# Nucleus search on one core: the next search's bracket inside the tie branch, the next logits' maxima after round two, and scaled results of S put into the attention groups

## The chip, the cores and the metric

The kernel runs on one core of one Trainium2 chip. The metric is device time in microseconds (us). An execution with the hardware profiler gives the trace; its own time is given beside its span.

## The reference, cut to what matters

Layer 0 is a graph attention over N = 2708 nodes with D = 512 features and 8 heads. Layer 1, which the change is about, runs two steps of a diffusion with three streams:

```
S = adj + I;  Rf = S / rowsum;  Rb = S / colsum
for s in (0, 1):
    logits = (Xa W1) W2 (Xa W3)^T                    # N x N
    order each row by falling logits; csum = cumulative softmax
    keep the first k_i = #(csum < 0.9) + 1 of the row  # "nucleus"
    A  = softmax of the kept logits, 0 elsewhere
    Xf = Rf Xf;  Xb = Rb Xb;  Xa = A Xa
    Z += Xf U1[s] + Xb U2[s] + Xa U3[s]
out = x + layernorm(X + Z) * gamma + beta
```

The kernel does not sort. For each row it searches for the threshold above which the sum of exp(logit - max) just reaches 0.9 of the total.

## The kernel before, in words

Rows lie in 22 tiles of 128 partitions, and two tiles make a pair, so a step has eleven pairs, 0 to 10. Two pairs make a quad. The two steps are the two passes of one outer loop; "step one" is s = 0, "step two" is s = 1 (`last` in the code).

For each pair the work runs through these stages.

- `Logits.products` (L534, L536): TensorE forms the logits of the pair in chunks, ScalarE copies each chunk from PSUM into the tile p. The pool holds four p tiles, two pairs, so the copies of pair g+2 wait until the search of pair g has finished with its p.
- `Logits.exp`: VectorE takes the rows' maxima (L561, two reductions over 2708 elements). It returns a list of further steps for ScalarE and GpSimd ("fills"): a sum with half the exponent (`root`), the exponential (`full`), three trial thresholds from these sums by GpSimd (`points`, L578-L588), and twelve passes of ScalarE over the rows (L566, "looks") that give the masses above the three thresholds; GpSimd puts them together (`masses`, L591-L593, the tile pts).
- `search`: VectorE forms a bracket around the threshold from the three masses (L637-L666, tiles g0, ends, below), then does rounds of a secant search, each with one pass over each row tile (L642): two in step one, four in step two. After that it picks out the next largest values (L819, L821), forms `keep` (the kept exponentials, L743 or L748-L751), and tests for ties.
- `branch`: the test's result is packed into the integer code_i (L900), loaded into a register of the VectorE queue (L901), and a switch of five arms follows (L903). Arm 0 is empty, arms 1 to 3 mend ties in one or both tiles (L760-L770), arm 4 does more rounds. After the switch stands the reciprocal rden (L920).
- `attended`: TensorE transposes keep in groups of four 128x128 blocks (L1069), ScalarE copies each group out of PSUM (tile at, L1073), TensorE multiplies by va (L1087), which holds Xa. A tile has six groups, a pair twelve. ScalarE scales the result by rden (L1095).
- In step one, `mixed` multiplies the result by U3 and writes it out. In step two GpSimd adds z to it (L1097), which holds what the other streams gave, and `normed` normalizes the rows: statistics by VectorE (L137, L138), two operations by VectorE (L1150, L1151) and a store on GpSimd's queue (L1152).
- `part` gives the products with S as a list of steps ("others"): in step one S by [Xf, Xb] (which start as the same X) and through U1 and U2; in step two S by the streams (L983), through U (L1004), and at the end of each half of a quad four calls of `summed`, one for each tile: ScalarE scales a PSUM bank into xe (L1027, two buffers), GpSimd adds that to z (L1029). The first half of a quad also loads z (SP's queue).

The order on TensorE, ScalarE, VectorE and SP is written out by hand; `paced(steps, n)` does the next n steps of a list. GpSimd's order is the scheduler's. Iteration g of the loop does the products of pair g+2, the attention of pair g on TensorE and ScalarE, the search of pair g+1 on VectorE, the fills of pair g+2 between the attention's groups, and part g+2 of the S products:

```
for g in range(-1, NP):
    others = part(half, g + 2)
    if g + 2 < NP: lg[g + 2].products()
    ...
    if g >= 0: att = attended(pairs[g], *ready, fills, others, ...)
    def early(g=g):                      # called by search after its first round
        if g + 2 < NP: fills.extend(lg[g + 2].exp())
        return lambda: [rest() for rest in norms] + [paced(pending, len(pending))]
    def late(g=g):                       # called by search before its selection
        if g >= 0: out_ = rest_of(att); ...
            while others or fills: paced(others, 2); paced(fills, 1)
    ready = search(lg[g + 1], g >= 0, early, late)
```

So the four results of `summed` are done at the end of an iteration, ahead of the next products.

Of the kernel before, what the change touches and what calls it, by code (L numbers as in the profile page):

```python
# [24 lines left out]
P = 128  # L25
LEAKY_ALPHA = 0.2
LN_EPS = 1e-5
P_NUC = 0.9
# [25 lines left out]
def kernel(  # L54
# [553 lines left out]
                steps.append(masses)  # L608
            return steps

    def search(lg, looked, early, late):
# [6 lines left out]
        tiles = [(i, rows[t]) for i, t in enumerate(grp)]  # L618
        junk = wide.tile([P, -(-N // 4) * 2], F32, name="junk", bufs=1)
        junk_b = junk.bitcast(BF16)[:, :N]  # L620
# [8 lines left out]
        ends = vec("ends", 2, 3)  # L629
        cur = vec("cur", 3)  # L630
        th = vec("th")
        g0 = vec("g0")
        if lg.ragged:
            v.memset(cur, 0.0)

        def aim(dst, th):
            v.scalar_tensor_tensor(dst, th, AIM[s], lg.cap, op0=OP.mult, op1=OP.min)  # L637
            v.scalar_tensor_tensor(dst, tot, 1.0 - P_NUC + CURVE, dst, op0=OP.mult, op1=OP.add)
            v.reciprocal(dst, dst)

        def mass(i, pr, th, dst):
            v.scalar_tensor_tensor(junk_b[:pr], ps_[i][:pr], th, ps_[i][:pr],  # L642
                                   op0=OP.is_ge, op1=OP.mult, accum_out=dst)

        if not looked:
            for j in range(NA):
                for i, pr in tiles:
                    mass(i, pr, lg.th[:pr, j, i:i + 1], lg.pts[:pr, j, 2, i:i + 1])
        aim(g0, lg.th[:, NA // 2])
        v.tensor_scalar(ends[:, 0, 1], tot, CURVE, None, op0=OP.mult)  # L650
        v.tensor_copy(ends[:, 1, 1], lg.top)
        v.reciprocal(ends[:, :, 1], ends[:, :, 1])
        v.tensor_tensor(ends[:, :, 1], ends[:, :, 1], g0.unsqueeze(1).to_broadcast([P, 2, G]), op=OP.subtract)
        v.memset(ends[:, 0, 0], X_LO)
        v.memset(ends[:, 1, 0], X_HI)
        v.tensor_copy(ends[:, 0, 2], tot)
        v.memset(ends[:, 1, 2], 0.0)
        pg = lg.pts[:, :, 1]
        v.tensor_tensor(pg, lg.top.unsqueeze(1).to_broadcast([P, NA, G]), lg.pts[:, :, 2], op=OP.subtract)
        v.reciprocal(pg, pg)  # L660
        v.tensor_tensor(pg, pg, g0.unsqueeze(1).to_broadcast([P, NA, G]), op=OP.subtract)
        below = vec("below", 2, NA, dtype=I32)
        for e, order, op in ((0, range(NA), OP.is_ge), (1, reversed(range(NA)), OP.is_lt)):
            v.tensor_scalar(below[:, e], pg, 0.0, None, op0=op)
            for j in order:
                v.copy_predicated(ends[:, e], below[:, e, j].unsqueeze(1).to_broadcast([P, 3, G]), lg.pts[:, j])  # L666
        side = vec("side", 2, dtype=I32)
        d = vec("d", 2)
        fr = vec("fr")

        def rounds(n, aim_at=None):
            for it in range(n):
                v.tensor_tensor(d, ends[:, 1, 0:2], ends[:, 0, 0:2], op=OP.subtract)
                v.tensor_scalar(d[:, 1], d[:, 1], -1e-12, None, op0=OP.min)
                v.reciprocal(fr, d[:, 1])
                v.tensor_mul(fr, fr, ends[:, 0, 1])
                v.tensor_scalar(fr, fr, -0.95, -0.05, op0=OP.max, op1=OP.min)
                v.tensor_mul(fr, fr, d[:, 0])
                v.tensor_tensor(cur[:, 0], ends[:, 0, 0], fr, op=OP.subtract)
                v.tensor_mul(th, cur[:, 0], cur[:, 0])  # L680
                v.tensor_mul(th, th, th)
# [203 lines left out]
        def branch(go):  # L885
# [8 lines left out]
            for q in range(4):  # L894
# [3 lines left out]
            v.scalar_tensor_tensor(flag_t[0:1, 0:G + 1], flag_t[0:1, 0:G + 1], 1.0, weights[0:1], op0=OP.mult,  # L898
                                   op1=OP.mult, accum_out=code[0:1])
            v.tensor_scalar(code_i[0:1], code[0:1], float(1 << G), None, op0=OP.min)  # L900
            what = nc.values_load(code_i[0:1, 0:1], engines=[DVE], min_val=0, max_val=1 << G,  # L901
                                  skip_runtime_bounds_check_because="at most 1 << G")
            for arm in tc.Switch({DVE: what}, (1 << G) + 1):  # L903
                if 0 < arm < 1 << G:
                    ties([x for x in tiles if arm >> x[0] & 1])
                elif arm == 1 << G and go == 0:
                    rounds(MORE_ROUNDS)
                    choose()
                    finish(1)
                elif arm == 1 << G and go == 1:  # L910
                    v.copy_predicated(th, short, vn[:, :, nx - 1])
                    v.copy_predicated(kept[:, 1], short, den)
                    finish(2)
                elif arm == 1 << G:
                    bisect()

        late()
        finish(0)
        rden = small.tile([P, G], F32, name="rden1")
        v.reciprocal(rden, den)  # L920
        return keep, rden

    big = ctx.enter_context(tc.tile_pool(name="big", bufs=1))
    va = big.tile([P, NT, D], F32, name="va")
# [2 lines left out]
    for s in range(STEPS):  # L927
        last = s == STEPS - 1
        with ExitStack() as st:
# [128 lines left out]
            def attended(grp, keep, rden, fills, others, first=3):  # L1058
# [94 lines left out]

                return rest

            def ranks():
# [5 lines left out]
                junk = wide.tile([P, -(-N // 4) * 2], F32, name="junk", bufs=1).bitcast(BF16)[:, :N]  # L1162
# [42 lines left out]
            pools = (wide, small, ps_t)  # L1205
            NP = len(pairs)
            with tc.manual_schedule(engines={PE, ACT, DVE, SP}):
                counted, spread = ranks() if last else (None, None)
                lg = [Logits(pools, s, grp, keys, rank) for grp in pairs[:1]]
                lg[0].queries()  # L1210
                lg[0].products()
# [9 lines left out]
                    step()  # L1221
                values()
                done = []
                ready = None
                looks = []
                for g in range(-1, NP):

                    fills = []
# [1 line left out]
                    others = part(half, g + 2)  # L1230
                    if g + 2 < NP:
                        lg[g + 2].products()
                    if g + 3 < NP:
                        lg.append(Logits(pools, s, pairs[g + 3], keys, rank))
                        lg[g + 3].queries()
# [17 lines left out]
                    def late(g=g):  # L1253
                        if g >= 0:
# [65 lines left out]
```

## Time and profile before

| | |
|---|---|
| median of 3 runs | 3685.08 us (3682.25 to 3693.7) |
| profiled execution | 3677.84 us, span 3676.0 us |
| busy, share of the span | PE 91%, DVE 72%, ACT 41%, POOL 24% |
| granted TensorE clock, mean | 0.962 |

PE is TensorE's matmul side, DVE VectorE, ACT ScalarE, POOL GpSimd, SP the queue of most loads. Layer 0 takes about the first 1090 us; step one's attention runs from about 1226 to 2300 us and step two's from about 2482 us on. A line such as "DVE nmx L561 <- ACT p L536" says that an instruction of line 561, which writes nmx, came to run when ScalarE's line 536 had written p; "issue" stands for time in which the engine waited for nothing that the profile shows.

### The profile page before, as it was taken

To read this page: it belongs to the slowest core of one execution; us is meant where nothing else is said; L and a number is where in the kernel's file an instruction comes from. 1 tells how busy PE (TensorE), PEld (TensorE's weight loads), DVE (VectorE), ACT (ScalarE), POOL (GpSimd) and SP (SyncE) were. 2 spreads that over 40 slices of the span, in tenths; PEclk is the share of its full clock that TensorE was granted. 3 is DMA by queue.
4 is the path that set the end of the run, shared out by engine and by line. 5 is a ranking of instruction groups with operands and counts; after the bars stand their busy time and mean duration, and the time that the engine had idled before them with its cause. 6 is when DMAs were issued, how large, how long until landed. Compare 5 with 4: busy or idle time off the path is not lost. (4 is left out here: it accounts for less than half of the span.)

```text
span 3676.0 us, 34194 instructions
## 1 busy us (share of the span) xinstructions
PE 3337.2 (91%) x10791; PEld 1723.9 (47%) x10791; DVE 2662.3 (72%) x4832; ACT 1504.8 (41%) x2248; POOL 873.0 (24%) x1072
## 2 busy tenths in 40 slices
PE   7998999998867799999999999879898999999887
PEld 4433333333444454646455553555455555555443
DVE  4587888989965557455464751887888998888884
ACT  2343212011113666565665641337444563545610
POOL 4114241514321012221122221311212222122211
PEclk9999999999979899999999999989999999999988
DMA  4476424233227344536254343874356444564442
GB/s 115 158 245 238 147 74 159 74 110 100 81 81 283 136 151 149 189 103 216 77 182 159 139 159 99 288 250 140 129 192 212 162 161 161 201 221 169 142 156 102
DMA packets 247978, 580.17 MB, mean 158 GB/s; under 512 B 33305, under 2 KB 67049, under 8 KB 243491
## 3 DMA queue, kind: packets, MB, share of 16 engines
q1 hardware_dynamic: 226695, 503.59, 41.0%
q0 software_dynamic: 21040, 73.88, 5.2%
q8 instruction: 86, 1.41, 0.2%
q14 instruction: 157, 1.29, 0.1%
HBM read 471.68 MB, written 105.68 MB: 157 GB/s over the span
## 5 line engine op out<-in xcount | busy, mean ns | idle before, releaser
L1087 PE MATMUL a<-va,at 128*128 128x512 f32 (+2 forms) x1936 | 893.5, 601 | 15.3 <-ACT at L1073 14.9
L442 PE MATMUL po<-e,fw 128*65 128x512 f32 (+4 forms) x2112 | 839.9, 553 | 34.2 <-DVE e L440 23.5
L440 DVE SCALAR_TENSOR_TENSOR e<-r_b,kk,a_c 128x512 f32<-128x512 f32 (+4 forms) x1056 | 751.3, 740 | 70.6 <-PE po L442 19.9
L566 ACT ACTIVATE junk_a<-p,nth 128x2708 uint8<-128x2708 f32 (+1 forms) x240 | 612.7, 2553 | 106.2 <-POOL nth L585 102.0
L983 PE MATMUL q<-hl,s_r 128*128 128x512 f32 x1936 | 524.1, 419 | 59.4 <-DMA s_r<-s_d 59.0
L442 PEld LDWEIGHTS po<-e,fw 128*65 128x65 f32 (+1 forms) x2112 | 285.8, 140 | 548.7 <-issue 270.5
L1087 PEld LDWEIGHTS a<-va,at 128*128 128x128 f32 (+2 forms) x1936 | 339.1, 187 | 390.0 <-issue 340.5
L983 PEld LDWEIGHTS q<-hl,s_r 128*128 128x128 f32 x1936 | 361.6, 191 | 211.9 <-issue 59.9
L642 DVE SCALAR_TENSOR_TENSOR junk<-p,th 128x2708 bf16<-128x2708 f32 (+1 forms) x132 | 409.7, 3103 | 3.8
L1004 PE MATMUL q<-u_k,tt 128*128 128x512 f32 x704 | 319.9, 597 | 9.6 <-DMA u_k<-in_L_gnn_U_dram 9.6
L1073 ACT COPY at<-t 128x512 f32<-128x512 f32 (+3 forms) x308 | 140.5, 477 | 438.9 <-PE t L1069 438.1
L986 PE MATMUL q<-s_r,hl 128*128 128x512 f32 (+1 forms) x1056 | 281.0, 410 | 10.9 <-DMA s_r<-s_d 10.7
L534 PE MATMUL t<-keys,q_t 128*128 128x452 f32 x528 | 166.8, 447 | 110.9 <-ACT p L536 97.4
L986 PEld LDWEIGHTS q<-s_r,hl 128*128 128x128 f32 x1056 | 186.7, 188 | 99.3 <-issue 52.0
L1004 PEld LDWEIGHTS q<-u_k,tt 128*128 128x128 f32 x704 | 134.8, 192 | 160.9 <-issue 156.7
L561 DVE TENSOR_REDUCE nmx<-p 128x1 f32<-128x2708 f32 (+1 forms) x44 | 129.6, 2969 | 99.1 <-ACT p L536 99.1
L821 DVE MAX8 vn<-keep 128x8 f32<-128x2708 f32 (+1 forms) x66 | 196.8, 2981 | 2.3
L536 ACT COPY p<-t 128x452 f32<-128x452 f32 (+2 forms) x264 | 132.7, 537 | 133.7 <-PE t L534 106.7
L534 PEld LDWEIGHTS t<-keys,q_t 128*128 128x128 f32 x528 | 94.9, 215 | 180.2 <-ACT p L536 153.0
L424 ACT ACTIVATE s_c<-a_c 128x512 fp32r<-128x512 f32 (+3 forms) x132 | 76.2, 577 | 244.9 <-DMA a_c<-in_adj_t_dram 118.6
L1127 PE MATMUL a<-u_k,v_t 128*128 128x512 f32 (+1 forms) x352 | 169.5, 618 | 1.9 <-DMA u_k<-in_L_gnn_U_dram 1.8
L1069 PE MATMUL t<-ident,keep 128*128 128x128 f32 (+1 forms) x968 | 147.8, 275 | 23.9 <-DVE keep L770 11.3
(305 smaller groups left out, 3362.3 us busy)
## 6 DMA issues: line engine op xcount, KB each, us to landing
s_r<-s_d SPq DMA_DIRECT2D x330, 256.0 KB
hl<-vhl_d SPq DMA_DIRECT2D x132, 512.0 KB
hl<-fhl_d SPq DMA_DIRECT2D x132, 512.0 KB
hl<-bhl_d SPq DMA_DIRECT2D x132, 512.0 KB
u_k<-in_L_gnn_U_dram SPq DMA_DIRECT2D x184, 256.0 KB
arow<-in_adj_dram SPq DMA_DIRECT2D x21, 1354.0 KB
s_d<-s_c SPq DMA_DIRECT2D x88, 256.0 KB
a_c<-in_adj_t_dram SPq DMA_DIRECT2D x84, 256.0 KB
```

The lines of the kernel that those rows point to most:

```text
L440: nc.vector.scalar_tensor_tensor(e[:pr, :cw], r_b[:pr, i, :cw], kk[:pr, t, hd:hd + 1], a_c[t][:pr, :cw], op0=OP.max, op1=OP.mult)
L442: nc.tensor.matmul(po[i][:, :cw], lhsT=fw[:pr, t, hd, :], rhs=e[:pr, :cw], start=(t == 0), stop=(t == NT - 1))
L534: nc.tensor.matmul(pl[:, :c1 - c0], lhsT=q[:, i], rhs=self.keys[:, c0:c1], start=(i == 0), stop=(i == 1))
L566: nc.scalar.activation(junk[:pr], self.p[i][:pr], func, **kw)
L642: v.scalar_tensor_tensor(junk_b[:pr], ps_[i][:pr], th, ps_[i][:pr], op0=OP.is_ge, op1=OP.mult, accum_out=dst)
L821: v.max(vs, keep[0][:pr])
L983: nc.tensor.matmul(half[j], lhsT=s_r[:, j * P:(j + 1) * P], rhs=hl[:, h], start=(c == 0 and h == 0), stop=(c == NT - 1 and h == 1))
L986: nc.tensor.matmul(half[j][:, :w], lhsT=hl[:, h, j * P:(j + 1) * P], rhs=s_r[:, :w], start=(c == 0 and h == 0), stop=(c == NT - 1 and h == 1))
L1004: nc.tensor.matmul(half[j], lhsT=across_t[-1][:, k, j * P:(j + 1) * P], rhs=u_k, start=(start and k == 0), stop=(start and k == KD - 1))
L1069: nc.tensor.transpose(pt[:rows[c], j, :pr], keep[i][:pr, cols[c]], ident[:pr, :pr])
L1087: nc.tensor.matmul(pa[:pr], lhsT=at[:rows[c], j, :pr], rhs=va[:rows[c], c, :], start=(c == 0), stop=(c == NT - 1))
L1127: nc.tensor.matmul(pz[i][:rows[t]], lhsT=v_t[i][:, k, :rows[t]], rhs=u_k, start=(k == 0), stop=(k == KD - 1))
```

## The change

Three edits, as the description of the change has them.

1. The tiles of the bracket move into a class `Opened`, in two parts: `ready` (the subtraction that needs the masses, and the curve at the middle threshold, g0) and `bracket` (all the rest). For pairs 2 to 10 `ready` of the next pair is issued between code_i and its load, and `bracket` at the end of each of the five arms. For pairs 0 and 1 both stay in front of the search. The small tiles get two buffers, and junk is allocated once a step.
2. `early` is called after round `s` rather than after round 0: in step two the next pair's maxima come after the second round, and with them the rest of `normed` moves ahead of the third round. In step one nothing moves.
3. In step two up to four last steps of `others` (the calls of `summed`) are left over at the end of an iteration, and the next iteration's attention does one of them in each of its groups from the second on.

```diff
+    class Opened:
+        def __init__(self, lg, looked, junk):
...
+            if looked:
+                self.ready()
...
+        def ready(self):
+            v, lg = nc.vector, self.lg
+            if lg.ragged:
+                v.memset(self.cur, 0.0)
+            pg = lg.pts[:, :, 1]
+            v.tensor_tensor(pg, lg.top.unsqueeze(1).to_broadcast([P, NA, G]), lg.pts[:, :, 2], op=OP.subtract)
+            self.aim(self.g0, lg.th[:, NA // 2])
+        def bracket(self):
...
+            for e, order, op in ((0, range(NA), OP.is_ge), (1, reversed(range(NA)), OP.is_lt)):
+                v.tensor_scalar(below[:, e], pg, 0.0, None, op0=op)
+                for j in order:
+                    v.copy_predicated(ends[:, e], below[:, e, j].unsqueeze(1).to_broadcast([P, 3, G]), lg.pts[:, j])
...
-                if it == 1 and begun:
+                if begun:
                     begun.pop()()
...
-                if it == 0 and aim_at is not None:
+                if it == s and aim_at is not None:
                     begun.append(early())
...
             v.tensor_scalar(code_i[0:1], code[0:1], float(1 << G), None, op0=OP.min)
+            opened = None
+            if go == 0 and then:
+                opened = then()
             what = nc.values_load(code_i[0:1, 0:1], engines=[DVE], min_val=0, max_val=1 << G,
...
                 elif arm == 1 << G:
                     bisect()
+                if opened:
+                    opened.bracket()
...
                     nxt = turned(*steps[n + 1]) if n + 1 < len(steps) else None
+                    if n:
+                        paced(left, 1)
                     if n >= first:
...
-                    rk_t = small.tile([NT, P], BF16, name="rk_t", bufs=1)
+                    rk_t = sp.tile([P, 2 * G * P], F32R, name="s_r").bitcast(BF16)[:NT, :P]
...
-                            while others or fills:
-                                paced(others, 2)
+                            keeps = min(len(others), len(quads[g // 2 + 1])) if last and others else 0
+                            while len(others) > keeps or fills:
+                                paced(others, min(2, len(others) - keeps))
                                 paced(fills, 1)
+                            left.extend(others)
+                            others.clear()
                             return
...
-                        ready = search(lg[g + 1], g >= 0, early, late)
+                        if g == 0:
+                            opened = Opened(lg[1], True, junk)
+                            opened.bracket()
+                        then = (lambda g=g: Opened(lg[g + 2], True, junk)) if 0 <= g < NP - 2 else None
+                        ready, opened = search(lg[g + 1], opened, junk, early, late, then)
```

More of the change, by code (lines that the diff above doesn't have):

```diff
@@ L609, in exp, with vec, aim, mass @@
             return steps
-    def search(lg, looked, early, late):
+    class Opened:
+        def __init__(self, lg, looked, junk):
+            _, small, _ = lg.pools
+            self.lg, self.looked = lg, looked
+            self.tiles = [(i, rows[t]) for i, t in enumerate(lg.grp)]
+            self.junk_b = junk.bitcast(BF16)[:, :N]
+            def vec(name, *shape, dtype=F32):
+                return small.tile([P, *shape, G], dtype, name=name, bufs=2)
+            self.ends = vec("ends", 2, 3)
+            self.cur = vec("cur", 3)
+            self.th = vec("th")
+            self.g0 = vec("g0")
+            self.below = vec("below", 2, NA, dtype=I32)
+            self.side = vec("side", 2, dtype=I32)
+            self.d = vec("d", 2)
+            self.fr = vec("fr")
+            if looked:
+                self.ready()
+        def aim(self, dst, th):
+            v, lg = nc.vector, self.lg
+            v.scalar_tensor_tensor(dst, th, AIM[lg.s], lg.cap, op0=OP.mult, op1=OP.min)
+            v.scalar_tensor_tensor(dst, lg.tot, 1.0 - P_NUC + CURVE, dst, op0=OP.mult, op1=OP.add)
+            v.reciprocal(dst, dst)
+        def mass(self, i, pr, th, dst):
+            p = self.lg.p[i][:pr]
+            nc.vector.scalar_tensor_tensor(self.junk_b[:pr], p, th, p, op0=OP.is_ge, op1=OP.mult, accum_out=dst)
+        def ready(self):
+            v, lg = nc.vector, self.lg
+            if lg.ragged:
[4 more added lines that the diff above has]
+        def bracket(self):
+            v, lg = nc.vector, self.lg
+            ends, g0 = self.ends, self.g0
+            v.tensor_scalar(ends[:, 0, 1], lg.tot, CURVE, None, op0=OP.mult)
+            v.tensor_copy(ends[:, 1, 1], lg.top)
+            v.reciprocal(ends[:, :, 1], ends[:, :, 1])
+            v.tensor_tensor(ends[:, :, 1], ends[:, :, 1], g0.unsqueeze(1).to_broadcast([P, 2, G]), op=OP.subtract)
+            v.memset(ends[:, 0, 0], X_LO)
+            v.memset(ends[:, 1, 0], X_HI)
+            v.tensor_copy(ends[:, 0, 2], lg.tot)
+            v.memset(ends[:, 1, 2], 0.0)
+            pg = lg.pts[:, :, 1]
+            v.reciprocal(pg, pg)
+            v.tensor_tensor(pg, pg, g0.unsqueeze(1).to_broadcast([P, NA, G]), op=OP.subtract)
+            below = self.below
+            for e, order, op in ((0, range(NA), OP.is_ge), (1, reversed(range(NA)), OP.is_lt)):
+                v.tensor_scalar(below[:, e], pg, 0.0, None, op0=op)
+                for j in order:
+                    v.copy_predicated(ends[:, e], below[:, e, j].unsqueeze(1).to_broadcast([P, 3, G]), lg.pts[:, j])
@@ L615, in search @@
+    def search(lg, o, junk, early, late, then=None):
         (wide, small, _), grp, ps_, tot, thr, s = lg.pools, lg.grp, lg.p, lg.tot, lg.thr, lg.s
@@ L617, in search @@
         nx = NEXT[s]
-        tiles = [(i, rows[t]) for i, t in enumerate(grp)]
-        junk = wide.tile([P, -(-N // 4) * 2], F32, name="junk", bufs=1)
-        junk_b = junk.bitcast(BF16)[:, :N]
+        begins = o is None
+        if begins:
+            o = Opened(lg, False, junk)
+            for j in range(NA):
+                for x in o.tiles:
+                    o.mass(*x, lg.th[:x[1], j, x[0]:x[0] + 1], lg.pts[:x[1], j, 2, x[0]:x[0] + 1])
+            o.ready()
+            o.bracket()
+        tiles, aim, mass = o.tiles, o.aim, o.mass
+        ends, cur, th, g0, side, d, fr = o.ends, o.cur, o.th, o.g0, o.side, o.d, o.fr
+        junk_b = o.junk_b
         keep = [wide.tile([P, N], F32, name="keep") for _ in tiles]
@@ L624, in vec @@
             return small.tile([P, *shape, G], dtype, name=name, bufs=1)
[L629 to L669, printed above, removed]
         def rounds(n, aim_at=None):
@@ L915, in branch @@
                     bisect()
+                if opened:
+                    opened.bracket()
+            if go == 0:
+                nxt.append(opened)
+        nxt = []
         late()
@@ L920, in search @@
         v.reciprocal(rden, den)
-        return keep, rden
+        return (keep, rden), nxt[0]
     big = ctx.enter_context(tc.tile_pool(name="big", bufs=1))
@@ L1154, in normed, with ranks @@
                 return rest
-            def ranks():
+            def ranks(junk):
                 same = wide.tile([P, N], F32, name="keep")
                 mask = wide.tile([P, N], F32, name="keep").bitcast(BF16)[:, :(NT + 1) * P]
-                junk = wide.tile([P, -(-N // 4) * 2], F32, name="junk", bufs=1).bitcast(BF16)[:, :N]
                 own = small.tile([P, NT], F32, name="own", bufs=1)
@@ L1207 @@
             with tc.manual_schedule(engines={PE, ACT, DVE, SP}):
-                counted, spread = ranks() if last else (None, None)
+                junk = wide.tile([P, -(-N // 4) * 2], F32, name="junk", bufs=1)
+                counted, spread = ranks(junk.bitcast(BF16)[:, :N]) if last else (None, None)
                 lg = [Logits(pools, s, grp, keys, rank) for grp in pairs[:1]]
@@ L1223 @@
                 done = []
-                ready = None
-                looks = []
+                ready = opened = None
+                looks, left = [], []
                 for g in range(-1, NP):
@@ L1232 @@
                         lg[g + 2].products()
+                    if g < 0:
+                        paced(left, len(left))
                     if g + 3 < NP:
```

## The prediction

> **What bounds the kernel now.** I read the stages first, then the waits by stage, then the timeline at the places where one pair of row tiles follows another. A step handles eleven pairs, 0 to 10. The table of stages (us, then busy time of each engine) for step one from its pair 2 on, for the head of step two, and for the rest of step two:
>
> ```profile
> 1330.00:2130.00 800.00, 770.85 (x2513) 419.45 (x2514) 445.71 (x948) 491.94 (x611) 149.49 (x242) 0.98 0.42 145
> 2475.00:2850.00 375.00, 330.61 (x1116) 197.02 (x1114) 313.36 (x588) 198.00 (x223) 72.52 (x76) 0.95 0.48 165
> 2850.00:3420.00 570.00, 532.37 (x1823) 316.99 (x1824) 484.55 (x909) 288.93 (x331) 142.72 (x129) 0.99 0.53 180
> ```
>
> Step one is TensorE's: PE is busy 96%, DVE 56%. In step two PE has 88%, then 93%, and DVE 84% and 85%. There the two hold each other: ScalarE may copy the products of pair g+2 (L536) only when search g has left its branch, since they reuse its p buffers, and search g+1 needs those copies for its maxima (L561). What PE and DVE wait for in step two (us in total, times, longest; from the waits of two windows, 2560 to 3450 and 2475 to 3520):
>
> ```profile
> PE t L534 <- ACT p L536: 48.1, 23, 14.5
> ```
>
> ```profile
> DVE rden L920 <- issue: 50.6, 8, 7.6
> DVE nmx L561 <- ACT p L536: 27.3, 8, 7.0
> DVE pts L659 <- POOL pts L593: 26.4, 1, 26.4
> ```
>
> PE's wait is not the same everywhere. Before attention of pair 1 PE stands 12.95 us, before pair 3 14.5 us: DVE is late (pair 3 has ties). Before pairs 2 and 4 to 8 it stands 2.7 to 5.1 us in all, and DVE had left its branch 2 to 15 us earlier. There ScalarE's four scaled results, which wait for POOL's adds, stand in front of the copies:
>
> ```profile
> 3180.15 1.27 ACT L1027 ACTIVATE xe<-q,cinv 128x512 f32<-128x512 f32 x2 [30.46 <-PE q L983]
> 3182.24 0.69 ACT L1027 ACTIVATE xe<-q,cinv 128x512 f32<-128x512 f32 x1 [0.83 <-POOL z L1029]
> 3183.46 0.69 ACT L1027 ACTIVATE xe<-q,cinv 128x512 f32<-128x512 f32 x1 [0.53 <-POOL z L1029]
> 3184.05 0.97 ACT L536 COPY p<-t 128x452 f32<-128x452 f32 x2
> ```
>
> Last, the branch. From the end of code_i to rden DVE sits idle, here 6.4 us (4.6 to 7.6 over the searches without ties):
>
> ```profile
> 3159.63 0.14 DVE L900 TENSOR_SCALAR code_i<-code 1x1 int32<-1x1 f32 x1
> 3166.16 0.17 DVE L920 RECIPROCAL rden<-den 128x2 f32<-128x2 f32 x1 [6.39 <-issue]
> ```
>
> The sequencer's own records split this: the load and the jump into arm 0 end at 3161.0 with a prefetch hint, 1.2 us after code_i; the exit jump follows at 3161.3, and 4.9 us pass. Where an arm ran ties for 17 us, rden came 0.8 us after it[...]. In step one the exit takes 3.3 us (1835.4 to 1838.7).
>
> [...]L659 took 1.24 us at 2712.98, beside POOL's z adds, and 0.16 us at 3169.01; POOL's L591 took 2.88 us beside search 7 and 0.20 us in step one.
>
> **The change part by part.**
>
> *The bracket in the arms.* It splits in two by the timeline at 3167.84 to 3171.11: the first point's curve and the subtraction of pts (L637-639, L659), 0.8 us, now ahead of the load of code_i; the rest, 2.6 us, in every arm. Pairs 2 to 10 of each step get it, so 18 branches. In arm 0 the rest is shorter than the exit's 3.3 to 4.9 us, so I take it as hidden: DVE saves 2.6 us a search. In a tie arm it saves nothing. The price is that everything that waits for the arm's end (the p copies) is let go 0.8 + 2.6 = 3.4 us later, and that the subtraction waits for POOL's masses (L593), which come after ScalarE's last look. That wait stood behind rden; now the branch stands behind it.
> In step one this costs at one place. Before attention of pair 1 the p copies follow the last look at once (1333.81), and the masses end at 1334.77. New chain: 1334.8 + 0.8 + 1.3 (load and jump) + 2.6 = 1339.5. PE loses 5.7 us, and in a stage that PE bounds it does not come back. Before pairs 2, 4, 6 and 8 the masses end 7.6 to 9.0 us ahead of the copies, against 4.7 us needed, or 7.1 where POOL's work slows the copies by mask (three of L666 took 3.12 us at 1846.85, instead of 0.58): nothing, by a margin of 0.5 us at the worst; the odd ones have 21 us. So +5.7, bounds +5 and +10.
>
> *The maxima behind round two* (step two alone). A round is 9.1 us (2755.81 to 2764.87). Where DVE waited for p (27.3 us) it now computes. That cover is worth nothing while PE bounds the pair, but at the head of step two DVE is the bound (158 of 175 us busy), and the gaps ahead of the maxima of pair 1 (2.7 and 1.2 us) go: -3.9.
> Late is then what hangs on it. The maxima end 6 us after round two, then L1150/L1151 of the finished rows (3.2 us), then POOL stores these rows. Read from the program's order, the store now stands on POOL's queue ahead of the first z add.
>
> *The scaled results in the attention groups.* One L1027 (0.69 us) goes to each of groups 1 to 4, with its z add on POOL and, for each first half, the z load on SP, behind q_t and xw. ScalarE idles 3.3 us in groups 1 and 2, 0.2 and 0.9 us in 3 and 4, so at most 0.5 us of delay, against 2 us that the copies of at are early. SP has nothing to load for PE between these groups, since products begin in group 6: nothing for the z loads, unless q_t or xw ahead of them waits, which I do not see. The copies of p no longer wait: per place I take what exceeds the steady 1.0 us of step one, so 2.6, 2.1, 4.1, 2.1, 1.7, 2.1 before pairs 2, 4, 5, 6, 7, 8.
> The new wait: xe has two buffers, so the third L1027 (group 3) waits for the first z add, that for POOL's store, that for the end of L1151. Where DVE leads PE, the add ends some 8.5 us after PE's first transpose (L1069) and the third copy is due at 13: free. Where DVE is late, before pairs 1 and 3, I count from rden: rows' statistics and aim 4.4, two rounds 16.2, maxima 6, L1151 3.2, store and add 2.1, copy 0.7, root 2.9, copy of at 0.6, so 36.1; PE wants that group 7.2 + 20.6 = 27.8 after rden. PE stalls 8 us, and 1.3 more in the next group: 9.4 each. Queued behind the third copy on ScalarE are the root, the copies of at, and through them PE. The trace of before has no such wait; its bounds are 0 and 12.8 (PE not ahead at all); I take 9.4.
>
> *The sum*, as PE's place against before, in us:
> - Step one +5.7. Head of step two -3.9, so DVE at +1.8.
> - Pair 1: let go 3.4 later, +5.2; stall 9.4, +14.6 (a 10 us wait of ScalarE for the maxima during pair 0 is under PE's 12.95). Pair 2: -2.6, +12.
> - Pair 3: DVE would come to code_i 7 us earlier (two brackets, 5.2; no z adds beside the bracket, 3.7; less 1.8). The masses, paced by PE, allow 3. The tie arm ends 3 earlier; then 2.7 of bracket, but no longer the 6.7 us from the arm's end (2834.6) to the copy (2841.2): -7. Stall 9.4: +2.4.
> - Pairs 4 to 8: -2.1, -4.1, -2.1, -1.7, -2.1: -9.7.
> - Pair 9: DVE now waits for the masses, which ended 3.7 us ahead of code_i; less 0.8: -2.9, and up to 5 more[...]. I take -5.5, so -15.
> - The last search keeps its length (the bracket moved from it into the arm before): -0.8. The tail is the same.
>
> So -16. The profiled execution had 3677.8 us, 3676.0 of span, and would have 3662; the median shown is 3685.1, 7.3 above it, so I forecast **3669 us**, -0.4%. About 0.3%, 11 us, is what a measurement of this kernel tells from no change.
>
> **Rivals.**
> 1. *No stall.* For it: the store's place on POOL may cost less than read. Then the stall before pair 3 goes (the one before pair 1 is absorbed by pair 3's wait): -16 - 9 = -25, 3660 us.
> 2. *The arm hides nothing*[...]. For it: the trace has no arm of 2.6 us. Against it: 0.8 us after the tie arm. Then pair 3 comes 5 us later and pair 9 about 3: -8, 3677 us: no change.
> 3. *Slower: the deferred adds stall ScalarE in every pair.* Place: the third L1027 before pairs 2 and 4 to 8. It decides when DVE ends round two more than 4.5 us later than PE's first transpose, which holds if the masses in front of the branch hold DVE back by more than I count; against it, DVE leads there by 2 to 15 us now. Six stalls of 6 us: -16 + 36 = +20, 3705 us.
>
> **How the numbers follow.** Forecast 0.45, rival 1 0.20, rival 2 0.20, rival 3 0.15. The forecast's own range is 3660 to 3678 (step one's bounds, pair 9's 5 us). Both tails over all: 3650 to 3692. Faster by over 0.3%: most of the forecast and of rival 1, some of rival 2: 0.60; within: 0.22; slower: 0.18.
>
> **What would show it.** Right: rden still 5 to 7 us behind code_i, with round one 2.6 us nearer to rden; no L1027 ahead of L536, and L534 waiting about 1 us before pairs 4 to 8; DVE's wait for L593 in front of the branch, PE 5 to 6 us later before pair 1 of step one; in attention of pairs 1 and 3 of step two a wait of PE for the copy of at near 8 us, ended by ScalarE behind POOL. Wrong: a time over 3692 us, stalls of group 3 in other pairs too, or rden further than 8 us from code_i.

## The result, and the profile after

The changed kernel takes 3674.94 us (median of 13 runs, 3669.59 to 3683.38); the kernel before takes 3685.89 us in the runs beside it (13 runs, 3681.56 to 3693.7). The ratio is 0.9970, 95% interval 0.9961 to 0.9978: **11 us faster, 0.3%**. The forecast was 3669 us, 16 us faster.

The two profiled executions say less than that. The one of after took 3675.58 us (span 3673.8), typical for it; the one of before was 8 us quicker than its median. The start of step two lies at 2306.8 us in before and at 2319.6 in after, and in kernels that leave all earlier work alone it lies between 2306.8 and 2318.3. So I count step two from its own first product (L534) to the end of the span: 1369.2 us before, 1354.2 after, **-15.0**. In step one, the time between the first transposes of pair 0 and pair 1 grows from 116.3 to 119.2, **+2.9**. Together -12, which agrees with the medians. One execution stands behind each such length: from pair 0's first transposes to the start of step two it is 1080.0 to 1086.4 us in the eight kernels that leave step one's order alone, so a few us between two lengths mean little by themselves.

Line numbers move with the edits. The copies of the transposed blocks (tile at) are L1073 in before and L1111 in after, the products with va L1087 and L1127, the scaled results L1027 and L1065, the z adds L1029 and L1067, the last step of the norm L1151 and L1191, rden L920 and L958.

The stages of after, same columns as for before (busy us of each engine, granted clock, DMA share, GB/s). The windows are the same clock times, so they hold slightly other work:

```profile
1330.00:2130.00 800.00, 763.35 (x2483) 415.34 (x2482) 434.46 (x934) 484.75 (x603) 136.00 (x246) 0.98 0.42 143
2475.00:2850.00 375.00, 331.05 (x1113) 195.31 (x1112) 308.81 (x576) 194.67 (x220) 84.57 (x72) 0.96 0.50 171
2850.00:3420.00 570.00, 531.24 (x1823) 317.07 (x1822) 510.14 (x948) 286.56 (x331) 150.40 (x133) 0.98 0.53 181
```

VectorE is now 89% busy in the last of them (510.14 of 570), 85% before. The waits of PE in step two (us in total, times, longest; 2560 to 3450):

```profile
PE a L1127 <- ACT at L1111: 31.2, 13, 16.7
...
PE t L534 <- ACT p L536: 7.8, 40, 0.2
```

The wait for the copies of p has gone from 48.1 to 7.8 us, as edit 3 is built to do. But 31.2 us stand at a place that had 4.9 before: the copies of the transposed blocks. Two stalls, at pairs 1 and 3, make 26 of them. A third of 11.34 us stands just ahead of this window, at pair 0, where ScalarE waits for the maxima:

```profile
2538.14 0.20 ACT L569 ACTIVATE nmx<-nmx 128x1 f32<-128x1 f32 x1 [16.05 <-DVE nmx L561]
```

The prediction had this one (a 10 us wait of ScalarE), and it takes the place of the 12.95 us that PE stood there for p before. VectorE's waits (2475 to 3520):

```profile
DVE rden L958 <- issue: 48.4, 9, 6.3
...
DVE ends L661 <- issue: 7.5, 7, 1.1
DVE nmx L561 <- ACT p L536: 0.3, 1, 0.3
```

The wait for the copies of p (last line) was 27.3 us. The first line was 50.6, and is 48.4: the branch costs what it did.

**The stall at pair 3.** ScalarE, then POOL, then PE (start, duration, what ran, idle time before it and its releaser):

```profile
2862.20 0.69 ACT L1065 ACTIVATE xe<-q,rinv 128x512 f32<-128x512 f32 x1
2865.59 0.59 ACT L1111 COPY at<-t 128x512 f32<-128x512 f32 x1 [2.70 <-PE t L1107]
2886.06 0.69 ACT L1065 ACTIVATE xe<-q,rinv 128x512 f32<-128x512 f32 x1 [19.88 <-POOL z L1067]
```

```profile
2884.04 0.68 POOL L1192 DMA_DIRECT2D out_dram<-yo  x1 [26.87 <-DVE yo L1191]
2884.74 1.28 POOL L1067 TENSOR_TENSOR z<-z,xe 128x512 f32<-128x512 f32 x1
```

```profile
2889.72 4.07 PE L1127 MATMUL a<-va,at 128*128 128x512 f32 x4 [16.69 <-ACT at L1111]
```

Read it backwards. PE waits 16.69 us for a copy of at; that copy stands on ScalarE behind the third scaled result and the root, and the third scaled result waits 19.88 us for POOL's first z add; the add stands on POOL behind the store of a finished row, and the store waits for L1191, which stands on VectorE behind the maxima. It is the chain that the prediction drew.

**The stall at pair 1** has almost the forecast size (9.25 against 9.4 us) but another cause. Here POOL had done its adds; ScalarE's root waits for the maxima themselves:

```profile
2641.61 0.20 ACT L569 ACTIVATE nmx<-nmx 128x1 f32<-128x1 f32 x1 [12.42 <-DVE nmx L561]
2641.84 2.55 ACT L566 ACTIVATE junk_a<-p,nmx 128x2708 uint8<-128x2708 f32 x1
```

```profile
2644.69 4.07 PE L1127 MATMUL a<-va,at 128*128 128x512 f32 x4 [9.25 <-ACT at L1111]
```

**The branch.** VectorE's timeline of the search of pair 6 of step two:

```profile
3169.97 0.14 DVE L930 TENSOR_SCALAR code_i<-code 1x1 int32<-1x1 f32 x1
...
3171.79 0.17 DVE L661 TENSOR_SCALAR ends<-sums 128x2 f32<-128x2 f32 x1 [1.07 <-issue]
...
3173.74 0.58 DVE L676 COPY_PREDICATED ends<-below,pts 128x6 f32<-128x6 int32 x3
3180.00 0.17 DVE L958 RECIPROCAL rden<-den 128x2 f32<-128x2 f32 x1 [5.68 <-issue]
```

The bracket runs in the arm, from 3171.79 to 3174.32. Then 5.68 us pass, where before 4.9 us passed between the jump out of the empty arm and rden. The bracket was moved in front of this time, not beside it. The sequencer's records fit this: the exit jump is issued at 3174.26, 0.1 us after the last short instruction of the bracket has begun, so nothing is left to run beside what follows the jump; e7 and e8 below test this reading. At pair 3, whose arm runs ties for 17 us, rden came 0.8 us after the arm's last pass before; now it comes 5.79 us after the last instruction of the bracket. So the tie arms have become dearer.

**Step one, pair 1.** The copies of p:

```profile
1340.86 0.97 ACT L536 COPY p<-t 128x452 f32<-128x452 f32 x2 [2.94 <-DVE ends L662]
```

The releaser is the second instruction of the bracket, not the arm's end: they are let go as the bracket begins. ScalarE had ended its last look 2.94 us earlier; that is the 2.9 us that PE loses.

### The profile page after: what moved, and what is told of

The parts are those of the page before. It is cut to its first block, busy times and chain, and to the rows that moved or that the text cites. A ratio compares the mean times of both kernels' runs of the same rounds, so it can differ in the third digit from the quotient of the medians.

```text
span 3673.8 us, 34163 instructions
## 1 busy us (share of the span) xinstructions
PE 3339.6 (91%) x10791; PEld 1725.2 (47%) x10791; DVE 2668.4 (73%) x4832; ACT 1499.2 (41%) x2248; POOL 867.6 (24%) x1072
## 5 line engine op out<-in xcount | busy, mean ns | idle before, releaser
L1127 PE MATMUL a<-va,at 128*128 128x512 f32 (+2 forms) x1936 | 900.7, 605 | 55.3 <-ACT at L1111 55.1
L1127 PEld LDWEIGHTS a<-va,at 128*128 128x128 f32 (+2 forms) x1936 | 341.6, 189 | 433.6 <-issue 346.1
L1042 PE MATMUL q<-u_k,tt 128*128 128x512 f32 x704 | 321.2, 599 | 10.6 <-DMA u_k<-in_L_gnn_U_dram 10.6
L1111 ACT COPY at<-t 128x512 f32<-128x512 f32 (+3 forms) x308 | 140.0, 476 | 466.8 <-PE t L1107 466.1
L534 PE MATMUL t<-keys,q_t 128*128 128x452 f32 x528 | 155.7, 420 | 73.0 <-ACT p L536 59.3
L1107 PEld LDWEIGHTS t<-ident,keep 128*128 128x128 f32 (+1 forms) x968 | 114.6, 140 | 111.1 <-issue 83.8
L1107 PE MATMUL t<-ident,keep 128*128 128x128 f32 (+1 forms) x968 | 147.5, 275 | 18.6 <-DVE ends L662 10.7
```

The lines of the kernel that those rows point to most:

```text
L534: nc.tensor.matmul(pl[:, :c1 - c0], lhsT=q[:, i], rhs=self.keys[:, c0:c1], start=(i == 0), stop=(i == 1))
L1042: nc.tensor.matmul(half[j], lhsT=across_t[-1][:, k, j * P:(j + 1) * P], rhs=u_k, start=(start and k == 0), stop=(start and k == KD - 1))
L1107: nc.tensor.transpose(pt[:rows[c], j, :pr], keep[i][:pr, cols[c]], ident[:pr, :pr])
L1127: nc.tensor.matmul(pa[:pr], lhsT=at[:rows[c], j, :pr], rhs=va[:rows[c], c, :], start=(c == 0), stop=(c == NT - 1))
```

## The experiments

All ratios are to the kernel before, run beside it on the same chip, each with its 95% interval. Before's medians there are 3685.89 us for after, 3688.51 for e1 to e4, 3686.24 for e5 to e8, 3686.16 for e9 and e10 and 3687.2 for e11 and e12; the groups of e1 to e12 ran on four chips, so between groups the ratios say more than the medians. A and B are the theory and the rival of the expectation printed with each run. "Step two" is the length from the first product to the end in the profiled execution, as above (before 1369.2, after 1354.2).

| | what | median us | ratio | step two |
|---|---|---|---|---|
| after | edits 1, 2, 3 | 3674.94 | 0.9970 (0.9961 to 0.9978) | 1354.2 |
| e1 | edit 3 alone | 3665.59 | 0.9944 (0.9930 to 0.9957) | 1351.5 |
| e2 | edit 2 alone | 3677.96 | 0.9971 (0.9961 to 0.9981) | 1354.5 |
| e3 | edit 1 alone | 3694.67 | 1.0021 (1.0013 to 1.0028) | 1376.1 |
| e4 | edits 1, 3 | 3668.22 | 0.9949 (0.9935 to 0.9963) | 1353.0 |
| e5 | edits 2, 3 | 3676.45 | 0.9972 (0.9962 to 0.9982) | 1359.2 |
| e6 | after, rows first | 3667.77 | 0.9950 (0.9937 to 0.9964) | 1349.7 |
| e7 | after, round one in the arms | 3657.68 | 0.9921 (0.9907 to 0.9934) | 1338.8 |
| e9 | e7 without edit 2, arms in step two only | 3663.86 | 0.9944 (0.9931 to 0.9957) | 1345.4 |
| e10 | e9, late maxima once | 3662.53 | 0.9935 (0.9922 to 0.9949) | 1350.8 |
| e11 | e1, late maxima in pairs 0 and 5 to 10 | 3668.03 | 0.9941 (0.9927 to 0.9955) | 1352.5 |
| e12 | e9, late maxima in pairs 0 and 5 to 10 | 3652.63 | 0.9898 (0.9883 to 0.9912) | 1331.8 |

### One edit at a time

**e1, edit 3 alone**, on the kernel before:

```
+                    if n:
+                        paced(left, 1)
...
-                            while others or fills:
-                                paced(others, 2)
+                            keeps = min(len(others), len(quads[g // 2 + 1])) if last and others else 0
+                            while len(others) > keeps or fills:
+                                paced(others, min(2, len(others) - keeps))
                                 paced(fills, 1)
+                            left.extend(others)
+                            others.clear()
```

> The kernel before with edit 3 alone: up to four scaled results of S put off to the next attention's groups. Theory A (the copies of p were late only because these results stood ahead of them): PE's wait for L536 before pairs 2 and 4 to 8 of step two falls from 2.7 to 5.1 us each to about 1, nothing new comes at pairs 1 and 3, because there the p copies (and so PE) come only after the branch; 12 to 15 us below before, so about 3671 us. Rival B (DVE holds these pairs, PE would wait for it elsewhere): the wait moves to the copies of at or stays, within 4 us of before.

0.9944: 23 us below before by the medians, where A had 12 to 15, and 9 to 12 us better than the whole change (by the two medians, or by their gains over before). A gave the sign and the place, not the size. Its profile shows PE's waits for p down to 22.3 us, and no wait for a copy of at over 3.8:

```profile
PE t L534 <- ACT p L536: 22.3, 34, 9.5
...
PE a L1089 <- ACT at L1073: 12.3, 14, 3.8
```

VectorE's wait for the copies of p went with them, from 27.3 to 1.7 us, though edit 3 touches no instruction of VectorE:

```profile
DVE nmx L561 <- ACT p L536: 1.7, 3, 0.8
```

**e2, edit 2 alone**:

```
-                if it == 1 and begun:
+                if begun:
...
-                if it == 0 and aim_at is not None:
+                if it == s and aim_at is not None:
```

> The kernel before with edit 2 alone: in step two the next maxima and the rest of the rows' norm come after round two. Theory A (it pays only at the head of step two, where DVE bounds, and the scaled results still stand ahead of the copies of p): 3 to 5 us below before, DVE's 27 us of waits for p gone, PE's waits for p unchanged. Rival B (ScalarE's root then waits for the maxima at pairs 1 and 3 and holds the copies of at): 5 to 15 us above before, with a new wait of PE for the copies of at.

0.9971: 10.6 us, at least twice what A gave. It takes the same wait off VectorE, by coming to the maxima later:

```profile
DVE nmx L561 <- ACT p L536: 3.9, 2, 2.7
```

That pays again behind the head, where A saw nothing: all of before's 27.3 us lie in the searches of pairs 6 to 9. Counted from step two's start and against before, code_i of pair 1 stands 10.0 us earlier, that of pair 5 only 4.4, that of pair 9 16.1. PE's waits for p fell too, from 48.1 to 35.4 us. B's new wait for the copies of at came at pair 0 alone (10.6 us), not at pairs 1 and 3 (3.1 us at most), and B's loss did not come.

**e3, edit 1 alone** (after, with both other edits taken back):

```
-                if it == s and aim_at is not None:
+                if it == 0 and aim_at is not None:
...
-                            keeps = min(len(others), len(quads[g // 2 + 1])) if last and others else 0
...
+                            while others or fills:
+                                paced(others, 2)
```

> The kernel before with edit 1 alone: the bracket in the arms. Theory A ([...]the arm hides nothing): rden 2.6 to 3.5 us further from code_i (8 to 10 us in step two), round one no nearer to code_i, 3 us lost at pair 1 of step one; 0 to 4 us above before. Rival B (the forecast of the record: the arm is hidden, each search 2.6 us shorter): the DVE-bound places gain, 4 to 8 us below before.

1.0021: slower, 6 us by the medians, a little more than A had. The forecast's picture of edit 1 (rival B here) is refuted. rden comes 7.7 to 9.8 us after code_i at pairs 2 and 4 to 8 of step two. Pair 1 of step one costs 119.1 instead of 116.3 us. Step two is 6.9 us longer, 5.3 of which are there by pair 3, whose tie arm now shows its exit.

### Pairs of edits

**e4, edits 1 and 3** (after with `it == 0` for `it == s`):

> The kernel after without edit 2: the maxima and the rest of the norm after round one again; edits 1 and 3 stay. Theory A (in the kernel after, the maxima behind round two make the stalls of PE for the copies of at: 9.25 us at pair 1 through ScalarE's root, 16.7 us at pair 3 through POOL's store and z add): the stall at pair 1 gone, that at pair 3 down by 9 us to 7 or 8, 4 us lost at the head of step two; 8 to 14 us below after, about 3663 us. Rival B (DVE is late at these places whatever the order, so that the waits come back as waits for p): within 4 us of after, 3671 to 3679 us.

0.9949: 7 us below after by the medians, just short of A's range and outside B's. The stall at pair 1 is gone, that at pair 3 is 4.9 us, and 7 to 8 us came back as waits for p before pairs 1 and 3. So the two stalls of after are edit 2's.

**e5, edits 2 and 3** (e1 with the edit of e2):

> The kernel before with edits 2 and 3, without the bracket in the arms. Alone, edit 2 gave -10 us and edit 3 -23 us. Theory A (they share one gain and meet at pairs 1 and 3: with the maxima behind round two, the put-off results and ScalarE's root hold the copies of at there, some 10 us each): 14 to 20 us below before, about 3670 us, with PE waiting 8 to 11 us for the copy of at at pair 3. Rival B (they add, since the stall in after came of the bracket in the arms): 28 to 34 us below before, about 3657 us, with no wait of PE for at over 4 us.

0.9972, no more than edit 2 alone. A is right that the two do not add: both remove one wait, VectorE's for p. It came out 6 us slower than A's 3670. PE stalls for the copies of at, 7.1 us at pair 1 and 14.1 at pair 3, without any bracket in an arm:

```profile
PE a L1089 <- ACT at L1073: 26.7, 15, 14.1
```

That answers B: edit 1 did not make the stalls.

### Mechanisms

**e6, rows first**: the rest of the norm goes ahead of the maxima.

```
-                if begun:
-                    begun.pop()()
+                if it == 1 and aim_at is not None:
+                    rowsdone()
...
```

> The kernel after, with the rest of the norm (L1190, L1191 and the store that follows on POOL) moved from behind the maxima to round two's start, ahead of its passes. Theory A (at pair 3 the third scaled result waits for POOL's z add, that for the store, that for L1191): ScalarE's 19.9 us wait for the z add goes below 5 us; PE's 16.7 us wait at pair 3 falls to 7 to 9 us, then held by the root behind the maxima; pair 1, which the maxima alone hold, keeps its 9 us; 5 to 9 us below after. Rival B (the maxima alone hold ScalarE at pair 3 too): stall and time as in after, within 3 us.

0.9950, 7 us below after, inside A's range. ScalarE's wait for the z add at pair 3 falls from 19.88 to 8.40 us, where A had under 5, and what follows takes over much of the rest (ScalarE):

```profile
2865.86 0.69 ACT L1062 ACTIVATE xe<-q,rinv 128x512 f32<-128x512 f32 x1 [8.40 <-POOL z L1064]
2874.34 0.20 ACT L569 ACTIVATE nmx<-nmx 128x1 f32<-128x1 f32 x1 [7.79 <-DVE nmx L561]
```

PE's stall falls to 13.1 us, not to 7 to 9 (that at pair 1 stays, 10.9). The store and the late maxima were two locks on one door: with the store earlier, the root waits for the maxima. The store is not out of the way either: both stores of the pair still stand on POOL ahead of the first z add (2860.55 and 2862.06, the add at 2862.61).

**e7, round one in the arms**: after, and behind the bracket a new method with the small operations of round one and its two passes; the round in `search` leaves them out.

```
                 if opened:
                     opened.bracket()
+                    opened.probe()
...
```

> The kernel after, with round one of the next search (its small operations and both passes, 3.0 us each) also in the arms, behind the bracket. Theory A ([...]a long instruction stands last in it, so that the sequencer reaches the jump early): rden about 1 us after the second pass and 14 to 16 us after code_i; a search 4 to 5 us shorter where DVE is late (pairs 1, 3, 9 and the last), nothing at pairs 4 to 8; 8 to 16 us below after. Rival B[...]: rden 5 to 6 us after the second pass, the time within 3 us of after.

0.9921, 17 us below after, just above A's range. VectorE, pair 5 of step two:

```profile
3053.66 3.04 DVE L648 SCALAR_TENSOR_TENSOR junk<-p,th 128x2708 bf16<-128x2708 f32 x1
3056.63 0.08 DVE L648 DVE_READ_ACCUMULATOR junk<-p,th 128x1 f32 x1
3058.14 0.17 DVE L982 RECIPROCAL rden<-den 128x2 f32<-128x2 f32 x1 [1.44 <-issue]
```

The exit jump is at 3053.77, 0.1 us after the second pass began; from the jump to rden it is 4.3 us as elsewhere, but 2.9 of them lie under the pass. Of the 18 searches, rden stands 0 to 2.3 us behind the pass, instead of 2.7 to 6.0 behind the bracket.

**e8, one pass in arm 0**, on the kernel before:

```
+                if arm == 0 and go == 0:
+                    v.scalar_tensor_tensor(junk_b, keep[0], 0.0, keep[0], op0=OP.is_ge, op1=OP.mult)
```

> The kernel before, with one added pass over 2708 elements (3.0 us, its result not used) as the only work of arm 0. Theory A[...]: rden about 1 to 2 us after the end of the pass, so 5 to 7 us after code_i as without it. Rival B[...]: rden about 5 us after the pass and 9 to 10 us after code_i in step two.

The same by itself, in step two's pair 4:

```profile
2951.76 2.98 DVE L905 SCALAR_TENSOR_TENSOR junk<-keep 128x2708 bf16<-128x2708 f32 x1 [1.28 <-issue]
2958.18 0.17 DVE L922 RECIPROCAL rden<-den 128x2 f32<-128x2 f32 x1 [3.43 <-issue]
```

Over the 20 searches without ties, rden comes 5.8 us after code_i on the mean; in before, with the arm empty, 5.7 us. A pass of 3.0 us moved rden by 0.1: theory A. It was not free otherwise: step two of this one execution (3700.08 us) is 10.6 us longer than before's, and before the last pair PE waits 13.5 us for the end of the pass, where it stood 8.0 us for the arm's exit. One run cannot weigh that.

### Put together

**e9**: e7 with `it == 0` again, and the arms used in step two alone.

```
-                        then = (lambda g=g: Opened(lg[g + 2], True, junk)) if 0 <= g < NP - 2 else None
+                        then = (lambda g=g: Opened(lg[g + 2], True, junk)) if last and 0 <= g < NP - 2 else None
...
```

> Edits 1 and 3 in a form made from the runs so far: round one of the next search stands in the arms too (as in e7), the arms carry this in step two alone (step one keeps bracket and masses' wait behind the branch), and the maxima come after round one again (edit 2 undone). Theory A (the stalls at pairs 1 and 3 are edit 2's, 3 us at pair 1 of step one are edit 1's, and both are independent of the exit that e7 hides): PE's waits for the copies of at below 5 us each at pairs 1 and 3, the interval between the first attention of pairs 0 and 1 in step one 116 instead of 119 us; 7 to 14 us below e7, about 3647 us. Rival B (DVE is late at pairs 1 and 3 all the same, and the stalls come back as waits for p): within 4 us of e7.

A fell: 0.9944, 6 us slower than e7, past B's 4 us too, though the two intervals just meet. A's parts came true one by one (115.9 us at pair 1 of step one; no wait for at over 3.2 us), yet the time did not. What B named is there: PE's waits for p are back at 21.5 us, against 7.8 in e7. A second thing was not named by either. A search that is 4 us shorter comes to its maxima before the copies of p are there, and VectorE waits for them (0.3 us in after, 15.9 in e7):

```profile
DVE nmx L561 <- ACT p L536: 24.0, 10, 4.9
```

e12, where PE's waits for p stay (23.7 us), shows that this second wait is on the path.

**e10**: `it == 1` in the search of pair 1 alone.

> e9 with the maxima behind round two at one place alone, during the search of pair 1 of step two, where DVE waits for the copies of p (head of step two). Theory A (edit 2 gains its 4 us only there): 2 to 4 us below e9. Rival B (round one in the arm or the wait of PE for p has already taken this gain): within 1.5 us of e9.

0.9935, 1.3 us below e9 by the medians: nothing that can be told from no gain, as B had it, but for a third reason. I had aimed at the wrong search: the maxima that wait for p at the head are those of pair 1, and the search of pair 0 takes them. VectorE's wait stayed (25.7 us).

**e11** and **e12**: e1 and e9 with the late order in the searches of pair 0 and of pairs 5 to 10.

```
+                if it == (0 if lg.grp in pairs[1:5] else s) and aim_at is not None:
```

> The kernel of e1 (edit 3 alone) with the maxima behind round two in the searches of pair 0 and of pairs 5 to 10 of step two only; pairs 1 to 4 keep them behind round one. Theory A (edit 2 pays twice: 4 to 6 us at the head of step two, and, while PE bounds pairs 5 to 8, it lets VectorE run up to a round, 9 us, further ahead of PE, which is worth 5 to 8 us when VectorE sets the end from pair 9 on; its price is the stalls at pairs 1 and 3 alone): 8 to 13 us below e1, about 3656 us, with code_i of pair 9 some 7 us earlier against PE's attention of pair 8. Rival B (the lead does not grow where PE bounds, since the masses hold VectorE): at most 5 us below e1, the head's gain alone.

> e9 (round one in the arms of step two, edit 3) with the maxima behind round two in the searches of pair 0 and of pairs 5 to 10 only. Theory A (as for e11; the stalls at pairs 1 and 3 are gone as in e9, the lead of VectorE at pair 9 comes back as in e7): 8 to 16 us below e9 and 4 to 12 below e7, about 3650 us. Rival B (VectorE cannot make up the lead in the five pairs that are left): the head's gain alone, 3 to 6 us below e9, no better than e7.

e11 fell: 0.9941, the same as e1 within the intervals. In e1 VectorE waits only 1.7 us for p, so there was nothing left to take; the order cost a new stall of 5.2 us at pair 4. In e12, where VectorE is quick and does wait for p, the same edit brings the wait from 24.0 to 8.7 us and the time to **3652.63 us, 0.9898**: 11 us below e9 and 22 below the change as made by the medians, 17 and 27 by the ratios. It is the best version that was run, though its interval still overlaps that of e7. Its waits of VectorE and PE in step two:

```profile
DVE nmx L561 <- ACT p L536: 8.7, 6, 2.6
```

```profile
PE t L534 <- ACT p L536: 23.7, 34, 9.3
...
PE a L1151 <- ACT at L1135: 9.3, 13, 2.9
```

## Why the prediction was right, point by point

The sign and the rough size were right. That the sum came so near was in good part luck: it got there by errors that cancelled, a gain from edit 1 in step two that was a loss, and gains from edits 2 and 3 that were larger than counted. In the table, the forecast's place of PE in step two is counted from the step's own start (its +5.7 of step one taken off), and the measured one is the first transpose of each pair against before:

| place | forecast | measured |
|---|---|---|
| step one, pair 1 | +5.7 | +2.9 |
| pair 0 of step two | -3.9 | -5.1 |
| pair 1 | -0.5 | -8.3 |
| pair 2 | +6.3 | +2.2 |
| pair 3 | -12.7 | -9.9 |
| pair 4 | -5.4 | +8.5 |
| pair 8 | -15.4 | -10.1 |
| pair 9 | -20.7 | -14.8 |
| end | -21.5 | -15.0 |

- **The bracket in the arms: the step that failed.** "In arm 0 the rest is shorter than the exit's 3.3 to 4.9 us, so I take it as hidden" is wrong. I compared durations, and should have asked when the jump is issued. The two tie arms of before ended in a pass of 3 us, with the jump recorded 0.1 to 0.2 us after its start and rden 0.8 and 0.1 us after its end; the bracket ends in instructions of 0.17 us. From exit jump to rden it is 2.7 to 6.0 us in after whatever the arm did. So rden came 8.3 to 10.2 us behind code_i in the searches of pairs 1, 2 and 4 to 8, not 5 to 7: past the 8 us that the prediction itself had named as a sign of being wrong. Alone, the edit made step two 6.9 us longer (e3). Rival 2 had named an arm that hides nothing. For this arm e3 shows it (rden 7.7 to 9.8 us behind code_i); with a long pass last in the arm, e7 and e8 show otherwise (rden 0 to 2.3 us behind the pass in e7).
- **The p copies** "let go 3.4 us later" was wrong too: they are let go at the bracket's start. That halved the loss in step one, and at pair 1 of step two the 3.4 us did not come (PE's first transpose stands 9.4 us behind code_i, 9.6 in before). The rest of the gain there is VectorE's: it reaches code_i of pair 1 8.1 us earlier, not 3.9. In before three short instructions at the end of that search (L845 to L847) took 1.16 to 1.19 us each beside GpSimd's z adds; in after, with no z add beside them, 0.12 to 0.16.
- **The maxima behind round two.** The gain at the head was right. What I had as cover ("worth nothing while PE bounds the pair") was on the path. From code_i of pair 8 to the end it is 283 to 291 us in before and in all twelve kernels of the table, while from PE's first transpose of pair 8 it is 249 to 264: VectorE's chain sets the end more nearly than PE's place, and its 27.3 us of waits for p, all in the searches of pairs 6 to 9, counted. Edit 2 alone was worth 10.6 us. Late was what I said would be late: the store, and the maxima themselves, which I had not given to the root at pair 1.
- **The put-off results.** PE's gain from pair 4 to pair 8 was 18.6 us; I had 10.0, since I counted only the gaps at L534. From 2980 to 3420 PE is busy 92.9% of a period of 114.4 us before and 95.9% of 109.7 after, so its idle time fell from 8.1 to 4.5 us a pair; its busy time fell by 1.1, with the clock at 1.00 instead of 0.99.
- **The stalls.** Pair 1: 9.25 for 9.4, which is luck, since the cause was another. Pair 3: 16.7 for 9.4, by the chain that was drawn. From rden to PE's matmul it took 35.3 us, as counted (36.1). But PE wanted the group 18.6 us after rden, not 27.8, for it began the attention 2.1 us before rden (2852.29), where I had it 7.2 after. About half of that is the step about the arm: rden came 5.8 us behind the arm's last instruction, not 0.8. The rest is the copies of p, which began at 2845.18, before the tie arm's own passes had ended.
- **Rivals.** Rival 1 (no stall) and rival 3 (a stall in every pair) did not happen: pairs 4 to 8 have none. Rival 2's arm that hides nothing did; its 3677 us lies 2 us from the measured time, the forecast's 3669 lies 6.

What stays open is why rden comes 2.7 us after the exit jump once and 6.0 the next time; nothing that was run tells these apart. Nor does a run show what this time is spent on: the runs show only how long it is and what it runs beside. That the bracket's short instructions keep the sequencer from reaching the jump earlier is my estimate, from where the jump stands in the records (3174.26, the bracket's end at 3174.32); e7 and e8 show only that with one long last instruction most of this time passes beside it (2.9 of 4.3 us in e7).

## What to carry to other kernels

To hide what follows an arm's exit jump, put a long instruction last in the arm, as in e7 (rden 0 to 2.3 us behind it); work that ended in short ones was only moved ahead of it (rden 2.7 to 6.0 us behind). Ask too what waits for the arm's end. Two edits that remove the same wait do not add, so try each alone: here one of three was worth nearly twice all of them (0.56% against 0.30%). When an engine is made faster, ask again what it will arrive early for: the late maxima cost 7 us where every pair had them (after against e4), and were worth 11 where pairs 1 to 4 were left out and VectorE was quick (e12 against e9).

## What the runs showed of the hardware

- The jump out of a switch arm (COMPARE_BRANCH) is recorded with 0.06 to 0.08 us, but the next instruction of VectorE's code runs 2.7 to 6.0 us after it in after (2.9 to 6.0 in before).
- That time passes beside an instruction that is already running: 2.9 of 4.3 us in e7, and in e8 a pass of 3.0 us moved rden by 0.1 us on the mean of 20 searches. In before's tie arm of pair 3 the jump is recorded at 2831.7, the last pass runs from 2831.58 to 2834.56, and rden comes at 2835.36.
